# Reordering the products of a quantized gated feed-forward inside one large fused kernel

## The chip, the cores and the metric

The kernel runs on one core of a Trainium2 chip. The metric is the device time of one execution in microseconds. A core has five engines that run side by side, each through its own instructions in a fixed order: TensorE (PE in the profile) multiplies matrices into PSUM banks, VectorE (DVE), ScalarE (ACT) and GpSimd (POOL) work on elements, and SyncE (SP) issues transfers. An instruction that waits for another engine, or for a transfer, holds up everything that is queued behind it on its own engine.

## The reference

Two layers, each of a sequence mixer `s` and a feed-forward with `g = silu(ffn)`, joined as `x + s * g`, on x of 2 x 512 x 512 in float32. The change lies in the feed-forward of the second layer, and beside it lie small preparations for the second mixer (a state space model with 128 heads).

```python
Wg, Wu, Wd = dequant(gate_q, gate_s), dequant(up_q, up_s), dequant(down_q, down_s)
gate_score = silu(einsum('bsh,ih->bsi', x, Wg))          # h 512, i 1792
return einsum('bsi,hi->bsh', gate_score * einsum('bsh,ih->bsi', x, Wu), Wd)
...
xn = _layernorm(x)
s = _L1_attn_ref(xn, ...)       # its dt: softplus of a projection; cumulative sums over 128 steps
g = silu(_L1_ffn_ref(xn, ...))
x = x + s * g
```

`dequant` multiplies integers by a scale per group of 128 inputs. The mixer's last product takes `out_proj_w` with its rows scaled by `gnorm_w`.

## The kernel before, in words

The kernel runs layer 0, then the feed-forward of layer 1, then the mixer of layer 1. Layer 0 is put in order by a scheduler; from the line `ordered.enter_context(tc.manual_schedule())` on, each engine executes its instructions in the order in which the program writes them. At the seam the scheduler may place instructions of layer 0 between the first ones of the feed-forward: so it is with `second_input` for the second sequence (normalisation at L196, transposes `xn1t` at L133, copies at L134), which the second sequence's tiles need.

*The feed-forward.* The 1792 inner features are cut into four blocks of 512, 512, 512 and 256. A block has tiles of 128 features for each of the two sequences (b), and two tiles make a pair (q). `load_block` loads integers and scales of gate (g), up (u) and down (d) weights on SP's queue into a ring of six buffers, and its `finish` dequantises them on DVE (L549). The loops run (q, b) = (0,0), (0,1), (1,0), (1,1) in each block; in block 0 the pairs with q = 0 are computed by `single_tiles`, all others by `pair_of_tiles`. When the pairs of a block are done, eight `pf` tiles (L893, four 128-row tiles of each sequence) multiply by the down weights and are added up in `gl` (tiles `g`, L901 and L903).

*Plain tiles.* `single_tiles` (L816) makes four groups of 128x512 results (two tiles, g and u), each of four matmuls, then ACT takes silu (L823) and DVE the product (L824). The trace counts each float32 matmul twice.

*Pairs of tiles.* `pair_of_tiles` computes a pair for gate and for up with seven half-size products in place of eight (Winograd's form of Strassen's method). `seven` names them 1 to 7: factors are quarters of weights and activations and sums of them (`sg`, `su` by `weight_sums` and `th` by `column_sums`, all on POOL, L483 and L472). A product is two matmuls of 128x256 (L509, `product`). Of each kind one PSUM bank `ps` (names pg, pu) holds two sums: 1, 6, 7 and 4 are accumulated in the left half and 5 and 3 in the right; product 2 goes to a bank `py` shared by g and u. Quarters of the result are numbered c = 0 to 3 (tile c // 2, half of the columns c % 2). They are taken from the running sum: c = 0 is product 1 plus 2, c = 1 the sum after 6 plus the right half with 3, c = 3 the sum after 7 plus the right half, c = 2 the sum after 4. ACT copies the left half after 1, 6 and 7 (L777, L789); DVE adds (L782, L791, L797). Then ACT takes silu of gate (L801 to L803) and DVE multiplies by up (L806). The order on PE is 1 5 (g), 1 5 (u), 2 (g), add, 2 (u), add, 6 6, 7 7, then 4 3 (g), 4 3 (u).

*Work beside it.* `side` is called twice in a pair, at its two yields, and after every second `pf` tile. One call takes the next piece of `prepare` (for the mixer: `hn` and transposes `ht` with their copies to hT, the projection `pdt`, softplus by a polynomial on DVE L655 to L667, cumulative sums by matmul `cs`, `cj` and `ct`, exponentials on ACT) and the next two pieces of `scale_out`: SP loads 128 rows of `out_wT` into `wop` (L730), DVE scales (L735), POOL's queue writes to `wo_d` (L736). The three buffers of `wop` let a piece be scaled two pieces after its load.

*Behind it.* `load_bc(0)` loads the weights `wbc` of the mixer's first projection (`pjbc`, L1011) at the end of block 0, into a room of one buffer. After the last block SP loads `wh`, `wg` and `wo`, and `head` starts the mixer with `pjbc` and then `pjh`.

Of the kernel before, what the change touches and what calls it, by code (L numbers as in the profile page):

```python
# [15 lines left out]
P = 128  # L16
D = 512
# [31 lines left out]
def fused_kernel(  # L49
# [488 lines left out]
    with ExitStack() as l1:  # L538
# [33 lines left out]
        def prepare():  # L572
# [27 lines left out]
            for b in range(B):  # L600
# [55 lines left out]
                nc.vector.reciprocal(v, v)  # L656
                nc.vector.tensor_tensor(u, u, v, ALU.mult)
                nc.vector.tensor_tensor(q2, u, u, ALU.mult)
                nc.vector.tensor_scalar(v, q2, 1.0 / 17, None, ALU.mult)
                yield  # L660
                for n in range(15, 1, -2):
                    nc.vector.scalar_tensor_tensor(v, v, 1.0 / n, q2, ALU.add, ALU.mult)
# [4 lines left out]
                nc.vector.tensor_copy(part(0), grouped(z))  # L667
                Af = row("q2", "Af")
# [52 lines left out]
        def scale_out():  # L721

            pieces = [divmod(i, GT) for i in range(NG * GT)]
            ts = {}
            for i in range(len(pieces) + 2):
                if i < len(pieces):
                    g, k = pieces[i]
                    ts[i] = tmp.tile([P, D], F32, tag="wop", name=f"wop{i}", bufs=3)
                    o0 = g * GW + k * P
                    nc.sync.dma_start(ts[i], out_wT[o0 : o0 + P, :])  # L730
                if i > 1:
                    g, k = pieces[i - 2]
                    t = ts.pop(i - 2)
                    ct = g * GT + k
                    nc.vector.tensor_scalar(t, t, gn[:, ct : ct + 1], None, ALU.mult)  # L735
                    nc.gpsimd.dma_start(wo_d[g][:, k, :], t)  # L736
                yield
# [17 lines left out]

        def pair_of_tiles(its, sums, b, name):

            f = {kind: seven(*sums[kind], xn1T[b], b) for kind in "gu"}
            ps = {kind: bank(f"p{kind}{name}", (P, 2, HD)) for kind in "gu"}
            py = None  # L760
# [7 lines left out]
            def multiply(kind, i):  # L768
                if i == 2:
                    product(py["gu".index(kind)], f[kind][i], kind == "g")  # L770
                else:
                    product(ps[kind][:, int(i in (3, 5))], f[kind][i], i == 1)

            for kind in "gu":
                multiply(kind, 1)
                multiply(kind, 5)
                nc.scalar.copy(quarter(kind, 0), ps[kind][:, 0])  # L777
            two = bank(f"py{name}", (P, 2, HD))
            py = [two[:, 0], two[:, 1]]
            for kind in "gu":  # L780
                multiply(kind, 2)
                nc.vector.tensor_tensor(  # L782
                    quarter(kind, 0), quarter(kind, 0), py["gu".index(kind)], ALU.add
                )
            yield
            for i, c in ((6, 1), (7, 3)):
                for kind in "gu":
                    multiply(kind, i)
                    nc.scalar.copy(quarter(kind, c), ps[kind][:, 0])  # L789
                    if i == 7:  # L790
                        nc.vector.tensor_tensor(  # L791
                            quarter(kind, 3), quarter(kind, 3), ps[kind][:, 1], ALU.add
                        )
            for kind in "gu":
                multiply(kind, 4)
                multiply(kind, 3)
                nc.vector.tensor_tensor(  # L797
                    quarter(kind, 1), quarter(kind, 1), ps[kind][:, 1], ALU.add
                )

            nc.scalar.activation(its[1][:, 0:HD], ps["g"][:, 0], AF.Silu)  # L801
            nc.scalar.activation(its[1][:, HD:], its[1][:, HD:], AF.Silu)
            nc.scalar.activation(its[0], its[0], AF.Silu)  # L803
            for c in (2, 3, 0, 1):
                x = ps["u"][:, 0] if c == 2 else us[c]
                nc.vector.tensor_tensor(quarter("g", c), quarter("g", c), x, ALU.mult)  # L806
# [24 lines left out]
        def side():  # L831

            next(pieces, None)
            for _ in range(2):
                next(scaled, None)

        sums = {}
        for n, (i0, iw) in enumerate(blocks):
# [10 lines left out]
            for q in range(ni // 2):  # L849
                for b in range(B):  # L850
                    two, name = its[b][2 * q : 2 * q + 2], f"{i0}{q}{b}"
                    if n == 0 and q == 0:
                        run = single_tiles(two, q, b, name)
                    else:
                        run = pair_of_tiles(two, sums, b, name)
                    for half in range(2):
                        next(run)
                        if n > 0 or q > 0:
                            side()
                    for _ in run:  # L860
                        pass
                    if n == 0 and q == 0 and b == 0:
                        for s in range(B):
                            column_sums(s, xn1T[s])
                    if q == 0 and b == (1 if n == 0 else 0):
                        w["d"] = fin["d"]()
                        if more:
                            nxt["g"] = load_block("g", n + 1)
                    if q == 0 and b == 0 and ni > 2:
                        ahead = {kind: weight_sums(kind, 1, f"{i0}_1") for kind in "gu"}  # L870
# [909 lines left out]
```

## Time and profile before

| | us |
| --- | --- |
| median of 3 runs | 2334.16 (2332.72 to 2335.03) |
| the profiled execution | 2329.24 |
| its span, first to last instruction | 2327.5 |
| PE, DVE, ACT, POOL busy in it | 2255.4, 1433.8, 1247.8, 1134.7 |
| first matmul of the feed-forward (L816) | 243.14 |
| first plain tiles of the second sequence | 269.49 |
| first `pf` of blocks 0, 1, 2, 3 | 316.65, 415.73, 511.76, 565.75 |
| first `pjbc` | 580.42 |

Times in the trace count from the start of the span. A timeline line has start, length, engine, source line, operation, output <- input, shape, count, and in brackets how long the engine had been idle and what released it. The length of a matmul is modelled, and matmuls overlap: their pace is read from one start to the next. A line of the waits has the waiting operation, what it waited for, the total, how often, and the longest. The granted clock is TensorE's, 1.00 at full speed; over the whole span it was 0.993.

### The profile page before, as it was taken

Reading aid. Unit: us, or ns where it says so; the run is one execution under the profiler, and the core shown is the slowest. Engines: PE = TensorE matmul, PEld = TensorE weight load, DVE = VectorE, ACT = ScalarE, POOL = GpSimd, SP = SyncE. Lnnn points to the kernel's source line nnn. Section 1 sums busy time; section 2 is a strip of 40 time slices with the busy share of each in tenths; the row PEclk is TensorE's granted clock in tenths of the full one; section 3 lists DMA queues with packets and bytes.
Section 4 is the critical chain, followed back from the end, with each engine's and each line's share of the span. In section 5 each row is a group of like instructions: output and inputs, shape, how many; then the busy total and the mean of one; then the engine's idle time right before and its main releaser. Section 6 shows DMA issues by size and latency. Waiting matters only on the chain.

```text
span 2327.5 us, 33414 instructions
## 1 busy us (share of the span) xinstructions
PE 2255.4 (97%) x11804; PEld 1598.1 (69%) x11804; DVE 1433.8 (62%) x2766; ACT 1247.8 (54%) x2688; POOL 1134.7 (49%) x995
## 2 busy tenths in 40 slices
PE   7989898999999999999999999999999999999998
PEld 4545457665557777777777777777777777777776
DVE  5263456643676666666667666666666676757663
ACT  3141224222676666666666575656666665666660
POOL 4151522233164554745654474547465554655475
PEclk9999999999999999999999999999999999999999
DMA  4021255564454444444544354544445454444452
GB/s 165 0 73 54 80 172 187 206 232 170 144 180 139 143 135 154 123 127 137 185 130 129 118 160 136 152 155 136 118 127 174 133 152 123 159 118 135 147 158 91
DMA packets 195510, 323.38 MB, mean 139 GB/s; under 512 B 17680, under 2 KB 129168, under 8 KB 192912
## 3 DMA queue, kind: packets, MB, share of 16 engines
q1 hardware_dynamic: 188944, 300.28, 42.3%
q0 software_dynamic: 6400, 20.98, 2.4%
q8 instruction: 94, 1.54, 0.3%
q14 instruction: 72, 0.59, 0.1%
HBM read 294.45 MB, written 26.74 MB: 138 GB/s over the span
## 4 chain that ended last, share of the span: by engine, by line
PE 87%; DVE 6%; ACT 4%; DMA 1%; issue 1%; POOL 1%; SPq 0%; DVEq 0%; ACTq 0%
PE pjh L1011 18%; PE of L1334 14%; PE gt L509 12%; PE py L1041 5%; PE pjbc L1011 5%; PE pn L1139 4%; PE pf L893 3%; PE py L1050 3%; PE sh L415 2%; PE pg L509 2%; PE ofy L1334 2%; PE gty L509 2%; PE px L1093 2%; PE gt L1011 2%; PE hu L304 2%; PE pu L509 2%
## 5 line engine op out<-in xcount | busy, mean ns | idle before, releaser
L1011 PE MATMUL pjh<-hT,wh 128*128 128x512 f32 x1024 | 467.5, 599 | 0.5
L1157 POOL TENSOR_TENSOR eb<-CT,eb 128x768 f32<-128x768 f32 x128 | 230.2, 1818 | 443.4 <-DMA eb<-ea_d 416.1
L1022 DVE SCALAR_TENSOR_TENSOR hid<-pjh,cw,hid 128x511 f32<-128x511 f32 (+2 forms) x384 | 286.9, 747 | 83.2 <-ACT hid L1017 74.1
L1011 PEld LDWEIGHTS pjh<-hT,wh 128*128 128x128 f32 x1024 | 187.8, 190 | 202.5 <-issue 200.3
L1117 ACT ACTIVATE cs<-cs,sl 128x128 f32<-128x128 f32 x1024 | 323.6, 388 | 1.0 <-DMA cs<-cs_d 1.0
L483 POOL TENSOR_TENSOR sw<-wg 128x256 f32<-128x256 f32 x114 | 84.1, 738 | 287.7 <-PE gt L509 287.6
L1132 DVE TENSOR_TENSOR cs<-de,CB 128x512 f32<-128x512 f32 x256 | 175.4, 685 | 77.2 <-ACT de L1131 77.2
L1017 ACT ACTIVATE hid<-pjh,cb,cw 128x512 f32<-128x512 f32 x128 | 99.2, 775 | 166.3 <-PE pjh L1011 166.3
L1131 ACT ACTIVATE de<-cs 128x512 f32<-128x512 f32 x256 | 154.0, 602 | 49.3 <-DVE cs L1132 43.2
L1041 PE MATMUL py<-cs,hc 128*64 128x128 f32 x2048 | 180.3, 276 | 0.0
L1348 DVE SCALAR_TENSOR_TENSOR acc<-of,rg,acc 128x256 f32<-128x256 f32 x192 | 92.1, 481 | 137.8 <-PE of L1334 137.1
L509 PE MATMUL gt<-th,sw 128*128 128x256 f32 x684 | 175.6, 379 | 0.0
L1461 POOL TENSOR_TENSOR y<-y,sgt 128x512 f32<-128x512 f32 x124 | 161.9, 1327 | 12.1 <-ACT sgt L1217 9.9
L1086 POOL TENSOR_TENSOR sums<-sums,sq 128x512 f32<-128x512 f32 x110 | 140.1, 1274 | 19.4 <-ACT sq L1082 15.7
L1050 PE MATMUL py<-eb,st 128*64 128x128 f32 x1536 | 149.1, 273 | 0.0
L1145 DVE SCALAR_TENSOR_TENSOR st<-st,sl,pn 128x64 f32<-128x64 f32 x512 | 103.8, 275 | 62.5 <-ACT st L1141 62.4
L509 PEld LDWEIGHTS gt<-th,sw 128*128 128x128 f32 x684 | 126.7, 190 | 21.4 <-issue 6.5
L1041 PEld LDWEIGHTS py<-cs,hc 128*64 128x64 f32 x2048 | 121.5, 137 | 15.4 <-issue 13.4
L736 POOL DMA_DIRECT2D wo_d<-wop x64 | 34.7, 546 | 196.1 <-DVE wop L735 195.7
L1070 DVE SCALAR_TENSOR_TENSOR y<-hid,Dcol,y 128x512 f32<-128x512 f32 x128 | 125.7, 982 | 4.5
L1334 PE MATMUL of<-wt,y 128*128 128x256 f32 x512 | 120.6, 379 | 0.0
L1206 ACT COPY sgt<-gt 128x256 f32<-128x256 f32 x171 | 63.4, 371 | 104.6 <-PE gt L509 104.6
(330 smaller groups left out, 4586.2 us busy)
## 6 DMA issues: line engine op xcount, KB each, us to landing
cs<-cs_d SPq DMA_DIRECT2D x128, 512.0 KB, 4.2
eb<-ea_d SPq DMA_DIRECT2D x256, 192.0 KB, 6.1
wh<-in_in_wT SPq DMA_DIRECT2D x64, 512.0 KB, 9.1
wg<-in_in_wT SPq DMA_DIRECT2D x64, 512.0 KB, 7.5
el<-ea_d SPq DMA_DIRECT2D x256, 128.0 KB, 7.5
wop<-in_out_wT SPq DMA_DIRECT2D x64, 256.0 KB, 2.8
wo_d<-wop POOLq DMA_DIRECT2D x64, 256.0 KB, 2.6
wo<-wo_d SPq DMA_DIRECT2D x16, 1024.0 KB, 8.7
```

Source lines behind the costliest of these rows:

```text
L509: nc.tensor.matmul(ps, x[:, k, :], y[:, k, :], start=(first and k == 0), stop=(k == 1), skip_group_check=True,)
L1011: nc.tensor.matmul(ps, w_of(k), hT[:, k, bass.ts(b, S)], start=(k == 0), stop=(k == KD - 1))
L1022: nc.vector.scalar_tensor_tensor(dst[:, j:], ps[:, : S - j], cw[:, ct, KCONV - 1 - j : KCONV - j], dst[:, j:], ALU.mult, ALU.add,)
L1041: nc.tensor.matmul(py[bass.ts(hh, HP), bass.ts(c, P)], hc[:, c, bass.ts(hh, HP)], M[:, hh, bass.ts(c, P)], start=True, stop=(c == 0),)
L1050: nc.tensor.matmul(py[bass.ts(hh, HP), bass.ts(c, P)], st[:, c - 1, bass.ts(hh, HP)], cte[:, hh, bass.ts(c - 1, P)], start=False, stop=True,)
L1086: nc.gpsimd.tensor_tensor(sums[u], sums[u], q, ALU.add)
L1117: nc.scalar.activation(m[:, bass.ts(c, P)], m[:, bass.ts(c, P)], AF.Relu, bias=sls[g][:, 3, b * NCH + c, h0 + hh : h0 + hh + 1], scale=-1.0,)
L1131: nc.scalar.activation(pe, m, AF.Exp, scale=-1.0)
L1132: nc.vector.tensor_tensor(m, pe, CBs[s // GT].rearrange("p c i -> p (c i)"), ALU.mult)
L1157: nc.gpsimd.tensor_tensor(eb_t[s], CTs[s // GT][:, P:].unsqueeze(1).to_broadcast([P, 2, S - P]), eb_t[s], ALU.mult,)
L1334: nc.tensor.matmul(ps, x[:, k, :], y[:, k, :], start=(first and k == 0), stop=(k == 3), skip_group_check=True,)
L1461: nc.gpsimd.tensor_tensor(y_of(s), y_of(s), sgs.pop(s), ALU.mult)
```

## The change

Products: 2 (g) and 2 (u) now follow each other, and 6 follows, before the adds that take `py`. Product 3 of a pair, with its add and the silu and multiply of quarter 1, moves into the next pair: its g part behind that pair's product 6, its u part behind its product 7. After a block's last pair both stand behind the first `pf` tile. Silu is taken quarter by quarter.

Order: block 0 runs (0,0), (1,0), (0,1), (1,1), with (1,0) computed by `single_tiles` too. The dequantisations of block 0's down weights and of block 1's gate weights now both stand behind (0,1).

Beside it: a pair has four yields, `side` is called at each and after every `pf` tile, and takes one piece of `scale_out` instead of two. `prepare` yields at more places. `scale_out` has five buffers, of which two lie in the room of `wbc`, and scales a piece four calls after its load. `load_bc(0)` moves to the end of the last block. Block 0's `column_sums` and `weight_sums` follow (1,0).

```diff
-                yield
                 for n in range(15, 1, -2):
+                    if n % 4 == 3:
+                        yield
                     nc.vector.scalar_tensor_tensor(v, v, 1.0 / n, q2, ALU.add, ALU.mult)
...
+            room = tmp.tile([P, 3, D], F32, tag="wop", name="wop")
+            more = wa.tile([P, KD, 2, NST], F32, tag="wbc", name="wop_more", bufs=1)
+            more = more.rearrange("p k j o -> p (k j o)").rearrange("p (i d) -> p i d", i=2)
+            slots = [room[:, i] for i in range(3)] + [more[:, i] for i in range(2)]
+            behind = len(slots) - 1
+            for i in range(NG * GT + behind):
+                if i < NG * GT:
+                    o0 = i * P
+                    nc.sync.dma_start(slots[i % len(slots)], out_wT[o0 : o0 + P, :])
+                if i >= behind:
+                    ct = i - behind
+                    t = slots[ct % len(slots)]
                     nc.vector.tensor_scalar(t, t, gn[:, ct : ct + 1], None, ALU.mult)
+                    g, k = divmod(ct, GT)
                     nc.gpsimd.dma_start(wo_d[g][:, k, :], t)
                 yield
...
+            def gated(c, dst=None):
+                q = quarter("g", c)
+                nc.scalar.activation(q, ps["g"][:, 0] if c == 2 else q, AF.Silu)
+                nc.vector.tensor_tensor(q, q, ps["u"][:, 0] if c == 2 else us[c], ALU.mult)
             for kind in "gu":
                 multiply(kind, 1)
                 multiply(kind, 5)
+                copy(kind, 0)
+            yield
             two = bank(f"py{name}", (P, 2, HD))
             for kind in "gu":
-                multiply(kind, 2)
-                nc.vector.tensor_tensor(
-                    quarter(kind, 0), quarter(kind, 0), py["gu".index(kind)], ALU.add
-                )
+                multiply(kind, 2, two[:, "gu".index(kind)])
+            for kind in "gu":
+                multiply(kind, 6)
+                copy(kind, 1)
+            for kind in "gu":
+                add(kind, 0, two[:, "gu".index(kind)])
+            gated(0)
+            if late:
+                late[0]()
             yield
+            for kind in "gu":
+                multiply(kind, 7)
+                copy(kind, 3)
+            if late:
+                late[1]()
+            late.clear()
+            for kind in "gu":
+                add(kind, 3)
+            yield
             for kind in "gu":
                 multiply(kind, 4)
+            gated(2)
+            gated(3)
+            def last(kind):
+                multiply(kind, 3)
+                add(kind, 1)
+                if kind == "u":
+                    gated(1)
+            late.extend([lambda: last("g"), lambda: last("u")])
             yield
...
+            order = [(q, b) for q in range(ni // 2) for b in range(B)]
             if n == 0:
+                order = [(0, 0), (1, 0), (0, 1), (1, 1)]
+            for q, b in order:
+                two, name = its[b][2 * q : 2 * q + 2], f"{i0}{q}{b}"
+                if n == 0 and (q, b) != (1, 1):
+                    run = single_tiles(two, q, b, name)
+                else:
+                    run = pair_of_tiles(two, sums, b, name)
+                for _ in run:
+                    if n > 0 or b > 0:
+                        side()
...
             if more:
                 ahead = sums = {kind: weight_sums(kind, 0, f"{i0}_2") for kind in "gu"}
             else:
+                wbc = {0: load_bc(0)}
                 wh = {q: load_hid(q) for q in range(2)}
...
-                    if r % 2 == 1:
-                        side()
+                    if b == 0 and r == 0:
+                        for f in late:
+                            f()
+                        late.clear()
+                    side()
```

## The prediction, on record before the result was known

> **What bounds the kernel now.** I read the page first (which engine is full, and which chain ends last), then the stage that the change touches, then what TensorE (PE) waits for there, then the two engines side by side around one such wait.
>
> The page's busy table and its chain that ended last:
>
> ```profile
> PE 2255.4 (97%) x11804; PEld 1598.1 (69%) x11804; DVE 1433.8 (62%) x2766; ACT 1247.8 (54%) x2688; POOL 1134.7 (49%) x995
> ...
> PE 87%; DVE 6%; ACT 4%; DMA 1%; issue 1%; POOL 1%; SPq 0%; DVEq 0%; ACTq 0%
> ```
>
> PE is the bound; DVE and ACT are on the chain only where PE stood waiting for them. The change touches only the quantized ffn, 243.14 us (first L816 matmul) to 579.64 us (end of the last L893). Busy time by stage of that stretch:
>
> ```profile
> 243.20:265.10 21.90, 13.85 (x34) 5.87 (x32) 19.92 (x31) 6.58 (x10) 14.72 (x12) 0.93 0.35 117
> ...
> 283.40:316.00 32.60, 27.08 (x116) 22.23 (x114) 14.14 (x30) 13.49 (x31) 2.17 (x4) 0.95 0.34 112
> 316.00:348.60 32.60, 32.60 (x113) 17.25 (x112) 21.14 (x32) 2.54 (x3) 10.14 (x14) 1.00 0.59 195
> 348.60:446.80 98.20, 90.58 (x386) 65.74 (x385) 64.00 (x118) 29.25 (x61) 26.93 (x40) 0.98 0.57 201
> 446.80:539.20 92.40, 84.94 (x337) 60.56 (x336) 44.69 (x90) 20.52 (x46) 26.98 (x42) 0.98 0.63 213
> ```
>
> Columns: stretch, its length, then busy us of PE, PE's weight loads, DVE, ACT, POOL, then granted clock and DMA. PE is short of its stretch, DVE is at two thirds. The ends of matmuls are modelled, so the loss is larger than these gaps. At its undisturbed pace a product of 128x256 takes a slot of 0.864 us (539.23 to 540.09 below), so a pair of 14 takes 12.10; a plain tile-kind 3.43; the eight `pf` tiles 27.47 (13.74 in the last block); hT transposes 3.46 in all, pdt 7.1, cs, cj and ct 10.7, xn1t 1.9. Before: 8 x 3.43 + 12 x 12.10 + 96.2 + 3.5 + 7.1 + 10.7 + 1.9 = 292.1 of 336.5 us. **44.4 us are excess**, and only that can be won. What PE waited for there:
>
> ```profile
> PE py L509 <- DVE it L782: 17.3, 12, 4.8
> PE xn1t L133 <- DVE acc L196: 8.1, 1, 8.1
> PE pg L509 <- DVE it L791: 3.7, 2, 2.7
> ```
>
> Twelve waits at `py` (one a pair), one for the second sequence's normalisation. An undisturbed pair, then a disturbed one, on PE:
>
> ```profile
> 539.23 1.03 PE L509 MATMUL pg<-xn1T,w_g 128*128 128x256 f32 x4
> 540.09 1.03 PE L509 MATMUL pg<-th,sg 128*128 128x256 f32 x4
> ...
> 542.68 1.03 PE L509 MATMUL py<-xn1T,w_g 128*128 128x256 f32 x4
> 544.29 1.13 PE L509 MATMUL py<-xn1T,w_u 128*128 128x256 f32 x4 [0.58 <-DVE it L782]
> ```
> ```profile
> 489.50 1.03 PE L509 MATMUL pu<-th,w_u 128*128 128x256 f32 x4
> 493.26 1.20 PE L509 MATMUL pg<-th,w_g 128*128 128x256 f32 x4 [2.74 <-DVE it L791]
> 494.26 1.91 PE L509 MATMUL pg<-xn1T,sg 128*128 128x256 f32 x4
> 495.96 1.84 PE L509 MATMUL pu<-th,w_u 128*128 128x256 f32 x4
> ```
>
> Even undisturbed, a pair takes 13.26 us (539.23 to 552.49), 1.16 over 12.10: 0.75 before the second `py` product and the rest at products 7 and 4. In the disturbed one the add that PE needs was queued on DVE behind two scalings that waited for their DMA:
>
> ```profile
> 487.18 0.42 DVE L782 TENSOR_TENSOR uq<-uq,py 128x256 f32<-128x256 f32 x1 [1.29 <-PE py L509]
> 491.34 0.49 DVE L735 TENSOR_SCALAR wop<-wop,gn 128x512 f32<-128x512 f32 x1 [3.74 <-DMA wop<-in_out_wT]
> 492.30 0.58 DVE L735 TENSOR_SCALAR wop<-wop,gn 128x512 f32<-128x512 f32 x1 [0.48 <-DMA wop<-in_out_wT]
> 492.81 0.40 DVE L791 TENSOR_TENSOR it<-it,pg 128x256 f32<-128x256 f32 x1
> ```
>
> So DVE's order, not its load, is the loss.
>
> **The change, part by part.**
>
> *First block.* (1,0) is computed plainly ahead of the second sequence: 13.73 us for a pair of 13.26. The instruction order of the changed kernel shows that only three of its sixteen matmul groups (3 x 0.86 = 2.6 us) come ahead of the xn1t transposes; PE arrives there at 256.87 + 2.6 = 259.4 and `acc` is unchanged at 265.1. The wait falls from 8.05 to 5.6 only, the 0.67 us wait for xn1T goes. Three groups of tiles end at 293.35 instead of 296.59: **-3.2**.
>
> *Pair order.* In the new pair both product-2 matmuls stand before the adds, so the 0.75 at `py` goes. Product 3 of the previous pair is put after 6 (g) and after 7 (u). That widens 6 to 7 and 7 to 4 by a slot. But DVE executes in order, and between 7 and 4 stand: add(u,1) of the previous pair (waits for 3u), its multiply, and only then add(g,3), for which 4g waits as it did before (L791 above). From the end of 3u's slot: DVE starts 0.20 later (399.66 to 399.86), add 0.46 to a dependent multiply (342.51 to 342.97, same length), 0.34 to an independent add (464.24 to 464.58), add 0.42, back to PE 0.05, restart 0.10: **about 1.5 us before 4g in every pair with a predecessor**, against 1.16 before. There are seven such pairs (three each in blocks 1 and 2, one in block 3); the first pair of a block pays 0.2, and its own product 3 goes into `pf`, where POOL's and SP's queues don't matter to it. I found no row of before with this order, so bounds: 0 if DVE takes add(g,3) unhindered, 3.7 if a scaling in the pieces ahead of it waits for DMA as at 491.34. I take 1.5, the sum of nearest rows.
>
> *Preparation in finer pieces, one scaling a call.* Pieces now come four times a pair and once a `pf` tile, before add(0), before add(u,1), before multiply(2) and at the end. What lies before add(0) has some 4.4 us of cover (product 2's adds aren't needed until copy 3, five slots on). What lies before add(u,1) has 2.2 us (end of 3g to end of 3u); beyond that it is PE's. Followed by hand with the rows of before (512-wide: tensor_tensor 0.69, scalar_tensor_tensor 0.72 each, reciprocal 3.35, scaling 0.44, dequantisation 2.28, hn 0.44, hT 0.64; ACT copy 0.37, four squares 2.45, table load 1.28):
> - block 0, last pair: sqrt of the first preparation, two dequantisations (4.56) and hn ahead of the first hT transpose: excess 2.0. All of v's chain falls under `pf`, with reciprocal and polynomial between `g` copies; six banks cover it. Before 296.59 to 348.57 = 52.0; now 12.1 + 1.7 + 3.6 + 27.5 + 2.0 = 46.8. **-5.2**.
> - block 1: pair (0,0) with cs, cj, ct: 0.3. (0,1): ACT has squares and two table loads ahead of copy(g,0), and hn behind the dequantisation: 3.3. (1,0): u, q2, v and a scaling, 2.3 us, in the narrow place: 3.0. (1,1): 1.5. The 3.0 gap also cools PE (below): 1.7. Sum 9.8 in place of 11.7: **-2.0**, unrounded. The second sequence's cs, cj, ct (5.35) move from block 2 into this `pf`; that is taken out of both sides.
> - block 2: 0.2 + 3 x 1.5 = 4.7 in place of 11.2 (2.80 and 2.74 waits, 1.7 cold): **-6.5**.
> - block 3: 1.7 for 2.5: **-0.8**.
>
> *Five buffers.* Load to scaling is now four calls instead of two half as dense ones. A slot's cycle is POOL issue 0.54, write 2.6, load 2.8, about 6 us, against four calls of about 3 us: the DMA wait on DVE should go (counted in block 2). Price: the weights `wbc` of the next stage share the room, so their two loads (8.6 us) move on SP's queue from block 0 to the end, behind the last scaling's write (call 68 of 78). That is at about 12 us into the last pair; they land some 7 us ahead of their first use (the `pf` of 13.7 plus product 3 follow). Behind them on SP wait `wh`, `wg` and `wo`; `wh0` is used 7 us after `wbc`, `wh1` waits for product 3 anyway, 19 us ahead of use. So nothing, and one us for each us if those 7 are used up. POOL's issues are as many as before.
>
> Sum -3.2 - 5.2 - 2.0 - 6.5 - 0.8 = **-17.7**: of the profiled execution's 2329.24 (span 2327.5) 2311.5 remain. The median of the runs is 4.9 above that execution, so **2316.5**.
>
> [...] After the 2.74 us gap, two products took 1.91 and 1.84 for 1.03: with the third 1.7 us lost, as after gaps of 4.83 and 3.30; after one of 2.80 nothing. [...] I take the rows. [...]
>
> **Rivals.**
> - *No gap before 4g* (DVE gets through add(g,3) in time): seven times 1.5 less, 2306.0. For it: DVE is at two thirds. Against it: its order in the built program.
> - *ACT and DVE hold each other*: silu(0), which waits for DVE's adds, now stands on ACT before copy(g,3); formerly all silus came last. One us more in each of eleven pairs: 2327.5. For it: block 1's DVE 64 of 98 us, in lumps. Against: five slots of slack.
> - *Slower*: the scaling before add(u,1) waits for its DMA in every late pair. At 2.5 us a time (17.7 / 7) the gain is gone, past 3.2 it is a loss; with 491.34's 3.74 each, 26.2 more: 2342.7. Against it: the 6 us cycle above in four calls.
> - *No change*: gaps merely move, 2334; only with both of the middle ones.
>
> **How the numbers follow.** Forecast 0.58, no gap 0.13, hold each other 0.18, slower 0.06, no change 0.05. The forecast's own range is 2310 to 2322 (0.9 us a late pair either way, the cold array, the wait for acc). Leaving out the far ends of the other cases gives 2305 to 2327. A measurement of this kernel tells about 0.2% (4.7 us) from no change: faster 0.88, same 0.06, slower 0.06.
>
> **What would show it.** Right: a wait of 5 to 6 us before xn1t; none for `py`; about 1.3 us shown before 4g (the `pg` product from `th`, after product 3u) released by DVE's add; wop scalings without DMA waits; the last `pf` ending 17 to 18 us earlier, `pjbc` following it within 1 us. Wrong: `pjbc` waiting for `wbc`, ACT copies releasing products 6 or 4, or 4g's waits well over 1.5 in block 2.

## The result, and the profile after

| | before | after |
| --- | --- | --- |
| median of 4 runs each, side by side (us) | 2333.44 (2331.70 to 2335.03) | 2318.32 (2316.73 to 2320.97) |
| ratio, with its 95% interval | 1 | 0.9936 (0.9919 to 0.9954) |
| profiled execution, span | 2329.24, 2327.5 | 2317.27, 2315.5 |
| the stage: first plain matmul to first `pjbc` | 337.28 | 324.36 |

The changed kernel is faster, by 15.1 us in the medians. In the profiled executions 12.0 us are gained: 12.9 in the stage, less 1.0 outside it.

Busy engines, and the head of the chain that ended last, on the page of the changed kernel:

```profile
PE 2249.6 (97%) x11780; PEld 1591.5 (69%) x11780; DVE 1434.6 (62%) x2758; ACT 1248.2 (54%) x2693; POOL 1135.3 (49%) x995
...
PE 89%; DVE 5%; ACT 4%; POOL 1%; issue 1%; DMA 0%; SPq 0%; DVEq 0%; ACTq 0%; POOLq 0%
```

DVE's and DMA's parts of the chain shrank by a point each, and nothing new entered it. The four blocks of the changed kernel follow (stretch, length, busy us of PE, weight loads, DVE, ACT and POOL, clock, DMA), and below them the list of what PE waited for:

```profile
243.65:341.27 97.62, 90.53 (x281) 49.20 (x280) 60.42 (x96) 26.67 (x46) 41.65 (x44) 0.97 0.42 139
341.27:444.10 102.83, 93.74 (x433) 70.33 (x432) 65.43 (x118) 35.22 (x74) 28.43 (x41) 1.00 0.65 221
444.10:526.95 82.85, 76.80 (x290) 54.38 (x288) 35.80 (x75) 15.49 (x41) 26.15 (x40) 1.00 0.58 192
526.95:568.01 41.06, 38.57 (x146) 27.00 (x144) 19.27 (x37) 11.62 (x28) 18.00 (x22) 1.00 0.53 183
```
```profile
PE pg L509 <- DVE it L785: 13.4, 10, 3.0
PE xn1t L133 <- DVE acc L196: 5.5, 1, 5.5
PE ht L626 <- DVE hn L619: 3.9, 5, 1.5
PE pg L509 <- ACT it L781: 1.2, 1, 1.2
```

The same cut of the kernel before has blocks of 105.43, 98.21, 92.45 and 41.19 us. The second sequence's `cs`, `cj` and `ct` (5.35 us of matmuls) lay in block 2 and now lie in block 1, so like for like the gains are 7.8, 0.7, 4.3 and 0.1 us. The wait for `py`, 17.3 us before, is gone. In its place ten waits stand ahead of product 4 (L785 is `add`), and these had been two. The end of a pair in block 2, on PE and then on DVE:

```profile
491.73 1.03 PE L509 MATMUL pg<-th,w_g 128*128 128x256 f32 x4
492.60 1.03 PE L509 MATMUL pu<-th,w_u 128*128 128x256 f32 x4
493.46 1.03 PE L509 MATMUL pu<-xn1T,su 128*128 128x256 f32 x4
495.95 1.10 PE L509 MATMUL pg<-th,w_g 128*128 128x256 f32 x4 [1.47 <-DVE it L785]
```
```profile
494.52 0.42 DVE L785 TENSOR_TENSOR uq<-uq,pu 128x256 f32<-128x256 f32 x1 [1.58 <-PE pu L509]
495.05 0.42 DVE L791 TENSOR_TENSOR it<-it,uq 128x256 f32<-128x256 f32 x1
495.39 0.42 DVE L785 TENSOR_TENSOR it<-it,pg 128x256 f32<-128x256 f32 x1
```

The third DVE line is add(g,3), which product 4 needs. Its own inputs were ready after product 7 of the gate; in front of it stand the previous pair's add(u,1), which waits for the moved product 3 (493.46), and that pair's multiply. This is the order that the prediction read off the program. Between the first matmuls of two such pairs lie 13.79 us.

### The profile page after: what moved, and what is told of

It is laid out like the page before. It is cut to its first block, busy times and chain, and to the rows that moved or that the text cites. A ratio compares the mean times of both kernels' runs of the same rounds, so it can differ in the third digit from the quotient of the medians.

```text
span 2315.5 us, 33350 instructions
## 1 busy us (share of the span) xinstructions
PE 2249.6 (97%) x11780; PEld 1591.5 (69%) x11780; DVE 1434.6 (62%) x2758; ACT 1248.2 (54%) x2693; POOL 1135.3 (49%) x995
## 4 chain that ended last, share of the span: by engine, by line
PE 89%; DVE 5%; ACT 4%; POOL 1%; issue 1%; DMA 0%; SPq 0%; DVEq 0%; ACTq 0%; POOLq 0%
PE pjh L1037 18%; PE of L1360 14%; PE gt L509 12%; PE py L1067 5%; PE pjbc L1037 5%; PE pf L916 4%; PE pn L1165 4%; PE py L1076 3%; PE sh L415 2%; PE ofy L1360 2%; PE gty L509 2%; PE px L1119 2%; PE pg L509 2%; PE pu L509 2%; PE gt L1037 2%; PE hu L304 2%
## 5 line engine op out<-in xcount | busy, mean ns | idle before, releaser
L1487 POOL TENSOR_TENSOR y<-y,sgt 128x512 f32<-128x512 f32 x124 | 161.9, 1327 | 12.4 <-ACT sgt L1243 10.5
L1095 DVE TENSOR_TENSOR y<-py,el 128x512 f32<-128x512 f32 x128 | 87.7, 685 | 51.7 <-PE py L1076 51.7
```

The lines of the kernel that those rows point to most:

```text
L1487: nc.gpsimd.tensor_tensor(y_of(s), y_of(s), sgs.pop(s), ALU.mult)
```

## Experiments

Whole times of different kernels differ by up to 8 us outside the stage, where their work is the same: span less stage is 1990.2 us before, 1991.1 after, 1997.9 in the first experiment. Of the 7.7 us between the kernel before and the first experiment 3.1 lie ahead of the stage (its first matmul at 246.19 for 243.14) and 4.7 behind it, where over the last 146 us of the span TensorE's granted clock is 0.98 in the one and 0.94 in the other. So each mechanism is judged on the length of the stage in the trace, with the whole time beside it. A stage length is one execution's, and matmuls at about half pace behind a wait (called cold below, the others warm) move it by 1.6 to 4.7 us from kernel to kernel. (In the kernel before, behind the wait of 4.83 us, two products started 1.71 us apart for 0.86, and the granted clock from 307 to 309 us was 0.50. In the experiments cold is said of the products' lengths and starts.) A difference of that size is told by the waits and not by the length alone. Each timed kernel ran beside the kernel before on its own chip; the ratio is to that. The changed kernel's ratio has the interval 0.9919 to 0.9954; those of experiments 1, 3, 4, 8 and 9 overlap it, so that their whole times alone don't part them from it.

**1. Adds of product 7 ahead of the late ones.** In the changed kernel only the order on DVE:

```diff
             for kind in "gu":
                 add(kind, 3)
+            if late:
+                late[2]()
+            late.clear()
...
-                add(kind, 1)
-                if kind == "u":
-                    gated(1)
+                if kind == "g":
+                    add(kind, 1)
+            def rest():
+                add("u", 1)
+                gated(1)
```

> Changed kernel, but on DVE the two adds of quarter 3 stand before the previous pair's add and multiply of quarter 1 (PE's order is untouched). Theory (the 1.47 us before product 4 come from DVE's order): the wait goes in block 2's three late pairs and block 3's one (4 x 1.6 = 6.5 us) and shrinks by about 0.9 in each of block 1's three; 2309, and no wait of PE for add(g,3) over 0.5 us in block 2's late pairs. Rival (DVE is simply too loaded there): 2318, the same waits.

Measured: 2313.70 us, ratio 0.9913 (0.9898 to 0.9928). The stage is 315.76 us, 8.6 less than after, and the pairs of block 2 with a predecessor come 12.09 us apart instead of 13.79. The waits of PE in this kernel, the first line of which had 13.4 us:

```profile
PE xn1t L133 <- DVE acc L196: 5.5, 1, 5.5
PE pg L509 <- DVE it L785: 4.2, 4, 2.0
PE ht L626 <- DVE hn L619: 3.9, 5, 1.5
PE pg L509 <- ACT it L781: 1.2, 1, 1.2
```

So the gap of the late pairs is DVE's order and nothing else. Of the stage's gain 4.6 us reached the median, which lies between the two expectations. The stretches outside the stage took more time here, as said above.

**2. The old order of block 0**, with everything else of the change left in (block 1's gate weights are dequantised behind (1,0) again):

```diff
-                order = [(0, 0), (1, 0), (0, 1), (1, 1)]
+                order = [(0, 0), (0, 1), (1, 0), (1, 1)]
-                if n == 0 and (q, b) != (1, 1):
+                if n == 0 and q == 0:
```

> Changed kernel, but block 0 in the order of before, (0,0), (0,1), (1,0), (1,1), the last two as pairs; preparation starts with (1,0). Theory: the wait before the transposes is 8.0 instead of 5.5 and 0.7 for their copies returns (+3.2), (1,0) takes 12.5 instead of 13.7 (-1.2), (1,1) has a late product 3 before it (+1.6): 2322. Rival (the order is of no account): 2317 to 2319.

Measured: 2339.57 us, ratio 1.0023 (1.0011 to 1.0034), a miss: slower than before. The stage is 343.50 us, and 18.3 of the 19.1 us over the changed kernel are block 0 (115.89 us). PE and DVE of this run, at the first of four waits of 3.9 to 5.4 us, two in block 0 and two in block 1:

```profile
297.43 2.07 PE L509 MATMUL pg<-th,w_g 128*128 128x256 f32 x4 [5.35 <-DVE it L785]
```
```profile
295.17 0.17 DVE L106 TENSOR_SCALAR ssh<-ssh 128x4 f32<-128x4 f32 x1 [1.92 <-ACT jkh L613]
296.69 0.18 DVE L108 RECIPROCAL ssh<-ssh 128x4 f32<-128x4 f32 x1 [1.35 <-ACT ssh L107]
296.95 0.42 DVE L785 TENSOR_TENSOR it<-it,pg 128x256 f32<-128x256 f32 x1
```

The preparation's square root, a chain between ACT and DVE, is inside a pair and stands ahead of the add that product 4 waits for. In the changed kernel the same chain begins beside a plain group, whose results nobody waits for so soon. (2.6 us of the loss are the wait before `xn1t`, which is 8.0 us again.)

**3. Product 3 back in its own pair**, ahead of the pair's end, all else left in:

```diff
-            late.extend([lambda: last("g"), lambda: last("u")])
+            for kind in "gu":
+                last(kind)
```

> Changed kernel, but product 3 with its adds and silu stays at the end of its own pair; product 2, pieces, buffers and block 0 as changed. Theory: a late pair takes 12.1 + 0.45 instead of 13.79, seven times 1.25 less: 2309.5; moving product 3 costs what the rest of the change wins. Rival (the moved product is what covers the copies and adds): products 7 and 4 wait again and it is slower than the changed kernel, 2322 to 2328.

Measured: 2319.87 us, ratio 0.9943 (0.9928 to 0.9958); stage 325.71 us. Neither expectation held. Blocks 2 and 3 gained 2.9 and 1.2 us, in the direction of the first (the last two pairs of block 2 take 12.6 us, its first two 14.1 and 13.2), but block 1 lost 5.7 us. There PE waited 1.81 us for a silu on ACT ahead of product 3, and 3.44 us ahead of product 4, and cold products of up to 2.07 us followed. Starts that lie 1.28 to 1.87 us apart for 0.86 make 4.7 of the 5.7 us. So this run doesn't show what the moved product is worth in block 1: that it fills waits there is likely, but most of the loss lies in cold products.

**4. The second sequence's transposes behind its turn.** `xn1t` of that sequence is taken out of `second_input` at the end of layer 0 and put behind (1,0), where PE has plain tiles to do until the normalisation is ready:

```diff
+                    for r in range(NCH):
+                        rt = (B - 1) * NCH + r
+                        features(acc[rt], xn1T[B - 1][:, :, bass.ts(r, P)], f"xn1t{rt}")
                     for s in range(B):
                         column_sums(s, xn1T[s])
```

> Changed kernel, but the four transposes of the second sequence and their copies are issued after all of (1,0) instead of within it. Theory: the wait of 5.5 us and the 1.8 us of cold clock behind it go, 0.7 us for the copies returns: 2311.7. Rival (what follows then waits for the transposed activations and their sums on POOL): 2316 to 2319.

Measured: 2315.65 us, ratio 0.9924 (0.9909 to 0.9938); stage 321.31 us. Block 0 gained 6.35 us, as expected, but block 1 gave 3.3 back, and the whole time lies between the two expectations. PE's waits in block 1 are the same ones; what differs is the pace of the products behind them. Two of its products in block 1 of this kernel, then the second one in the changed kernel:

```profile
368.62 2.04 PE L510 MATMUL pg<-th,w_g 128*128 128x256 f32 x4 [0.95 <-DVE it L786]
...
389.18 2.04 PE L510 MATMUL pg<-th,w_g 128*128 128x256 f32 x4 [2.99 <-DVE it L786]
391.02 1.76 PE L510 MATMUL pu<-th,w_u 128*128 128x256 f32 x4
```
```profile
393.96 1.10 PE L509 MATMUL pg<-th,w_g 128*128 128x256 f32 x4 [2.99 <-DVE it L785]
394.90 1.03 PE L509 MATMUL pu<-th,w_u 128*128 128x256 f32 x4
```

**5. Both edits, 1 and 4.**

> The two edits that each gained alone, together: in every pair the adds of products 7 stand on VectorE ahead of the second add and the multiply of the pair before, and the transposes of the second sequence's input stand behind its plain tiles. If the two gains are of different places (waits of 1.1 us before product 4 in blocks 2 and 3 here, the 5.5 us wait of the transposes there) they add: the stage from the first plain tile to the last product of the ffn measured 324.4 us in the changed kernel, 315.8 and 321.3 with the one and the other edit, and the second's own gain in block 0 was 6.4 us, of which block 1 gave 3.3 back through colder products; together 309.4 us if block 1 gives nothing back and 312.7 us if it gives the same back. The whole time is then 2303 to 2311 us, the width being the last 146 us, which scattered by 4 us between kernels that are the same there. Rival: the waits are covers of each other, and the stage stays at 315 us or more.

Measured: 2303.24 us, ratio 0.9864 (0.9847 to 0.9880). The stage is 307.69 us, even below the 309.4 expected: the two gains are of different places, and block 1 gave nothing back. It is 1.6 us shorter than in experiment 1, where the same wait of 2.04 us was followed by cold products. Experiment 1, and then this one:

```profile
394.71 1.29 PE L509 MATMUL pg<-th,w_g 128*128 128x256 f32 x4 [2.04 <-DVE it L785]
395.79 1.91 PE L509 MATMUL pu<-th,w_u 128*128 128x256 f32 x4
```
```profile
385.40 1.13 PE L510 MATMUL pg<-th,w_g 128*128 128x256 f32 x4 [2.04 <-DVE it L786]
```

**6. The same, and silu and multiply of quarter 0 behind the adds of product 7.**

```diff
             for kind in "gu":
                 add(kind, 0, two[:, "gu".index(kind)])
-            gated(0)
...
             for kind in "gu":
                 add(kind, 3)
+            gated(0)
             if late:
                 late[2]()
```

> As the one with both edits, and the silu and the multiply of quarter 0 moved behind the adds of products 7. In the first pair of block 2 that multiply stood on VectorE ahead of the add that product 4 waits for, and waited itself for a silu behind a table load of 1.28 us (wait before product 4 there 1.65 us); if that is the cause, this wait goes, and the one of 2.0 us in block 1's third pair, where the silus of the pair stand in the same place, falls by 0 to 1.5 us: the stage is 1.6 to 3.2 us shorter than with both edits alone, about 307 us. Rival: the wait is of ScalarE's copies for product 7, and stays; the stage is the same within 0.5 us.

Measured: 2300.61 us, ratio 0.9855 (0.9840 to 0.9870), the fastest kernel of this study and well under the changed one, whose interval it doesn't touch. The stage is 305.47 us, 2.2 less. Block 2 gave 1.6 of it, where the first pair went from 12.28 us to 10.68. In block 1 the third pair's wait fell from 2.04 to 0.69 us, but in the second pair product 6 now waits 3.23 us for a copy of ACT instead of 1.16, with a product of 2.07 us behind it, and block 1 as a whole stayed the same, 99.5 us for 99.3. So in block 2 the multiply was the cause, and not ACT's copies as the rival had it; in block 1 a wait for ACT, with the cold products behind it, took back what had been gained.

**7. One line alone: both products 2 ahead of their adds**, in the kernel before:

```diff
             for kind in "gu":
                 multiply(kind, 2)
+            for kind in "gu":
                 nc.vector.tensor_tensor(
```

> The kernel before with one line of the change alone: both products 2 of a pair stand ahead of their two adds, so that the second product does not wait for the add of the first, which reads the other half of the same bank. The kernel before waits 17.3 us in all for py; by hand, what is not met again by the next wait is 4.0 us in block 0, 2.3 in block 1, 2.4 in block 2 and 1.5 in block 3, 10 us in all: 2323 to 2325 us. It would mean that the larger part of what the change gains comes from this order alone. Rival: the adds then end as late as they did, and the waits only move on to products 7 and 4: 2331 to 2334 us.

Measured: 2332.18 us, ratio 0.9982 (0.9971 to 0.9992); stage 334.74 us, 2.5 less than before. The rival is right: the wait moved on. PE's waits for `py` are gone and stand ahead of product 4 instead. The list of this run, and then DVE ahead of the longest one:

```profile
PE pg L509 <- DVE it L792: 20.0, 6, 7.0
PE xn1t L133 <- DVE acc L196: 8.1, 1, 8.1
```
```profile
491.06 0.49 DVE L735 TENSOR_SCALAR wop<-wop,gn 128x512 f32<-128x512 f32 x1 [6.70 <-DMA wop<-in_out_wT]
492.00 0.49 DVE L735 TENSOR_SCALAR wop<-wop,gn 128x512 f32<-128x512 f32 x1 [0.45 <-DMA wop<-in_out_wT]
492.40 0.42 DVE L792 TENSOR_TENSOR it<-it,pg 128x256 f32<-128x256 f32 x1
```

DVE stood 25.7 us in all for the transfers of pieces, against 9.2 before. Why is not shown; that the scalings are reached sooner when PE is through products 2 sooner is the author's guess.

**8. The changed kernel with three buffers** for the pieces:

```diff
-            slots = [room[:, i] for i in range(3)] + [more[:, i] for i in range(2)]
+            slots = [room[:, i] for i in range(3)]
```

> The changed kernel with three buffers for the pieces of the output weights where it has five, each scaled two calls after its load. From load to scaling there are then about 10 us in the pairs' pace, against a transfer of 6 us or so in the trace; VectorE waits for a piece where a pair's calls come closer, and the adds behind it come late by as much: 2319 to 2323 us, if the five buffers do anything. Rival: with one piece a call the transfers are landed anyway, and the time is that of the changed kernel, 2318 us (within 1.5).

Measured: 2324.87 us, ratio 0.9953 (0.9939 to 0.9968); stage 328.51 us, 4.2 more. The median is above what either view expected, but its ratio's interval overlaps the changed kernel's. DVE waits 8.2 us for pieces, in five places, yet PE's waits are those of the changed kernel within 0.4 us (13.5, 5.5, 4.3 and 1.2 us). Of the 4.2 us 3.4 are in block 1, and they follow the same waits of 0.95 and 3.00 us, with products of 1.94 and 2.04 us behind them where the changed kernel has 1.10. So beside pieces that come one a call, five buffers took nothing off PE's waits. Most of the difference in the stage is one of that pace; whether the buffers have a part in how it fell was not tested. (A piece lands 2.8 us after its issue in the kernel before, in the median, and 2.8 or 2.9 in the changed one, where the expectation has 6.)

**9. Both products 2 ahead, and five buffers**, in the kernel before: experiment 7 with `scale_out` of the change, two pieces still scaled in a call, and `load_bc(0)` at the end.

```diff
+            slots = [room[:, i] for i in range(3)] + [more[:, i] for i in range(2)]
+            behind = len(slots) - 1
...
             for kind in "gu":
                 multiply(kind, 2)
+            for kind in "gu":
                 nc.vector.tensor_tensor(
```

> The kernel before with both products 2 ahead of their adds, and with five buffers for the output weights' pieces, two pieces still scaled in one call. With the order of products 2 alone the wait only moved: PE waited 20.0 us before product 4, and ahead of three of those six waits VectorE stood for a transfer of a piece (2.30, 3.89 and 6.70 us). If those transfers are what the gain was lost to, the five buffers give them two calls more to land, these three waits (4.19, 2.84 and 7.01 us) fall by 9 to 13 us with the colder products behind them, the stage goes from 334.7 to 322 to 326 us, and the time to 2320 to 2324 us. Rival: the two scalings and the multiplies ahead of the add of product 7 fill VectorE anyhow; the waits fall by less than 5 us, and the time is 2328 us or more.

Measured: 2314.94 us, ratio 0.9905 (0.9889 to 0.9922); stage 319.05 us. The buffers gained 15.7 us on top of the 2.5 of the product's order, more than the 9 to 13 us expected. The two together are already at least as good as the whole change (0.9905 against 0.9936). The buffers without the product's order were not run, and `load_bc(0)` moved with them, so how the 18.2 us are shared is not shown. No wait of DVE for a piece is left. PE's list has two waits of 5.8 us for DVE ahead of product 4 in place of six of 20.0:

```profile
PE xn1t L133 <- DVE acc L196: 8.0, 1, 8.0
PE pg L509 <- DVE it L793: 5.8, 2, 4.8
```

**10. The order of block 0 alone**, in the kernel before: (1,0) as plain tiles ahead of the second sequence, with the pairs, pieces and buffers as they were. As in the change, block 1's gate weights are loaded behind (0,1) and dequantised there at once, where the kernel before had a pair in between.

```diff
-            for q in range(ni // 2):
-                for b in range(B):
+            order = [(q, b) for q in range(ni // 2) for b in range(B)]
             if n == 0:
+                order = [(0, 0), (1, 0), (0, 1), (1, 1)]
```

> The kernel before with one part of the change alone: the first sequence's tiles of block 0 ahead, three plain groups, and one pair in that block; pairs, pieces and buffers as before. The changed kernel without this part was 21 us slower than with it, where the prediction gave the part 3.2 us and the shorter wait of the transposes. If the part is worth that much by itself, because preparation then begins beside plain tiles, which wait for nobody on VectorE: 2313 to 2318 us. If it is worth that only together with the finer pieces (which run into the pairs without it): 2328 to 2331 us, as the prediction's sum had it, 2331 minus up to 2.5 us for the transposes. Block 0's length in the trace tells: 105.4 us before, 97.6 us in the changed kernel, 115.9 us in the changed kernel without the part.

Measured: 2343.16 us, ratio 1.0033 (1.0024 to 1.0043): a miss of both, slower by 8 us. Stage 347.40 us, block 0 111.55. SP's queue (start, length until the last of the group was issued), DVE and PE of this run show how:

```profile
271.81 28.70 SPq L730 DMA_DIRECT2D wop<-in_out_wT  x4
300.61 0.38 SPq L545 DMA_DIRECT2D q_g<-in_gate_qT  x1
301.08 0.46 SPq L546 DMA_DIRECT2D w_g<-in_gate_sT  x1
```
```profile
309.18 2.29 DVE L549 TENSOR_TENSOR w_g<-q_g,w_g 128x2048 f32<-128x2048 int32 x1 [9.10 <-DMA w_g<-in_gate_sT]
311.39 0.41 DVE L782 TENSOR_TENSOR it<-it,py 128x256 f32<-128x256 f32 x1
```
```profile
311.86 2.08 PE L509 MATMUL py<-xn1T,w_u 128*128 128x256 f32 x4 [13.60 <-DVE it L782]
```

Four loads of pieces are issued beside (0,1), for three buffers. The fourth waits for the first to be scaled and written, and block 1's gate weights, which are behind it on SP, are asked for at 300.61 instead of 272.94 as in the changed kernel. DVE waits for their scales, and PE for DVE.

**11. Parts 7, 9 and 10 together:** products 2, five buffers and the order of block 0, with neither product 3 moved, nor pieces finer, nor silu in quarters.

```diff
+            order = [(q, b) for q in range(ni // 2) for b in range(B)]
             if n == 0:
+                order = [(0, 0), (1, 0), (0, 1), (1, 1)]
...
+            slots = [room[:, i] for i in range(3)] + [more[:, i] for i in range(2)]
...
+            for kind in "gu":
                 nc.vector.tensor_tensor(
```

> The kernel before with three parts of the change: products 2 ahead of their adds, five buffers, and the first sequence's tiles of block 0 ahead. With three buffers that last part cost 10 us, and the trace of that run shows where: on the DMA queue of SP the fourth load of a piece stood 28.7 us for a free buffer, and the load of block 1's gate weights behind it, so that VectorE stood 9.1 us for the weights' scales and TensorE 13.6 us for VectorE. With five buffers the four loads of that stretch find room. If that was all, block 0, 101.4 us with the two other parts, gains 2.6 us at the transposes (wait of 8.0 us to 5.5) and up to 1.7 us at the last pair's waits, and pays 1.6 us for a plain group where a pair was: 97.5 to 99.5 us, and the time is 2311 to 2313 us. Rival: the part costs by itself (preparation begins later and runs into block 1's pairs): block 0 at 101 us or more or block 1 longer by over 3 us, the time 2315 us or more.

Measured: 2311.58 us, ratio 0.9900 (0.9883 to 0.9916); stage 314.72 us, block 0 97.03. As expected (block 0 came out 0.5 us under its range): with room for the pieces, the order that cost 10.1 us of stage alone gains 4.3.

**12. The same, with the transposes of experiment 4.**

> The kernel before with the same three parts, and the transposes of the second sequence's input behind its plain tiles: the best that was found without moving product 3 and without finer pieces, to set against the best with them (2300.6 us, stage 305.5 us, which has the adds of products 7 ahead and the multiply later besides). The transposes gained 6.4 us in block 0 in the changed kernel; here the same: stage 308.4 us, 2302 to 2306 us. If it comes to that, moving product 3 and the finer pieces are worth no more than 3 us even where they are mended. Rival: what the transposes gain is given back in block 1 through colder products, as it was in the changed kernel (3.3 us): stage about 311.5 us, 2305 to 2310 us.

Measured: 2304.91 us, ratio 0.9878 (0.9861 to 0.9896); stage 308.65 us, as expected, with block 0 5.9 us shorter and nothing given back.

The stage lengths in one table, each from one profiled execution:

| kernel | block 0 | 1 | 2 | 3 | stage |
| --- | --- | --- | --- | --- | --- |
| before | 105.43 | 98.21 | 92.45 | 41.19 | 337.28 |
| products 2 (7) | 104.33 | 96.40 | 94.51 | 39.50 | 334.74 |
| and five buffers (9) | 101.36 | 95.73 | 82.46 | 39.50 | 319.05 |
| and block 0's order (11) | 97.03 | 95.73 | 82.47 | 39.49 | 314.72 |
| and the rest: the change | 97.62 | 102.83 | 82.85 | 41.06 | 324.36 |
| and adds first (1) | 97.72 | 100.96 | 77.73 | 39.35 | 315.76 |
| and late transposes (5) | 91.28 | 99.32 | 77.73 | 39.36 | 307.69 |
| and the multiply later (6) | 90.70 | 99.46 | 76.14 | 39.17 | 305.47 |

(In the rows from the change on, 5.35 us of `cs`, `cj` and `ct` lie in block 1 instead of block 2.)

Three of the change's parts make 22.6 us of gain, and the rest takes 9.6 back, of which the order on DVE that experiment 1 mends is 8.6. Where product 3 stays at home, pairs take 12.41 us in experiments 9 and 11, so the gap that it was moved to cover is 0.3 us once DVE is free; moved, they take 13.79. (Cold products have a part in these sums: behind the wait of 4.81 us in block 1, experiments 9 and 11 have them, the first of 2.01 and 1.95 us, while the changed kernel has none in block 1.) Mended, with the adds first, the rest comes to about nothing (315.76 against 314.72; with late transposes 307.69 against 308.65).

## Why the prediction was right, and where it was not

The forecast was 2316.5 us and the median is 2318.3, for the predicted reason, but the agreement is a little luckier than the working. The prediction took 17.7 us off the stage and 4.9 us from the profiled execution to the median. The stage gave 12.9, the rest of the program cost 1.0, and the median lay 1.1 above its profiled execution. Errors of 4.8 and 1.0 us one way and 3.9 the other leave 1.9.

*Pair order.* Right in kind and size: no wait for `py`, and a gap before product 4 of the gate (4g) in all seven late pairs. It measured 1.69 us a pair in block 2 (13.79 less 12.10) where the prediction took 1.5 (the rows that it lists add up to 1.57). Experiment 1 shows the cause, DVE's queue: with the adds ahead, those pairs take 12.09 us. The rival without a gap put 10.5 us on it; with that one order changed the stage came 8.6 us shorter and the median to 2313.7.

*The first pair of a block.* Mis-sized: 0.2 us was predicted and block 2's first pair lost 1.9 (12 products of 0.864 are 10.37, the pair took 12.28). With 0.19 more in each of the three late pairs this is all that is missing in block 2: 4.3 us gained, 6.5 predicted. Block 3 has the same two terms, at 0.1 us gained for 0.8: its first pair lost 0.5 us, its late pair 1.7, and its pairs before had lost 2.3 us where 2.5 were counted. In block 2, ACT of the changed kernel, then DVE, then PE:

```profile
451.60 1.28 ACT L790 ACT_TABLE_LOAD   x1
```
```profile
453.34 0.43 DVE L791 TENSOR_TENSOR it<-it,uq 128x256 f32<-128x256 f32 x1 [3.04 <-ACT it L790]
453.69 0.48 DVE L738 TENSOR_SCALAR wop<-wop,gn 128x512 f32<-128x512 f32 x1
454.08 0.41 DVE L785 TENSOR_TENSOR it<-it,pg 128x256 f32<-128x256 f32 x1
```
```profile
454.55 1.13 PE L509 MATMUL pg<-th,w_g 128*128 128x256 f32 x4 [1.65 <-DVE it L785]
```

The multiply of quarter 0 waits for a silu, whose table ACT has just had to load, and add(g,3) is queued behind it. The stage has 18 table loads, each of 1.28 us, where the kernel before has 17. The prediction named ACT's order as a rival, one us in each of eleven pairs; it did not follow the multiply into DVE's queue, ahead of the add. Experiment 6 moved it, and that pair came to 10.68 us.

*Block 0.* 7.8 us for the 8.4 of two steps. The sum was right, but what it gives for one part holds only beside the others. The loop order, costed at 3.2 us, is worth 4.3 of stage on top of experiment 9, minus 10.1 alone, and 19.1 inside the finished change. The prediction looked at PE's side of that step. The 10.1 us lost come from SP's queue, which had no free buffer (experiment 10), and the 19.1 from preparation that stands inside pairs on DVE (experiment 2), so the step can't be costed without the buffers and without where preparation starts. The wait before `xn1t` was right, 5.5 us for 5.6; experiment 4 shows that the whole of it was to be had.

*Block 1.* 0.7 us gained for 2.0. Pair by pair over its undisturbed length: (0,0) 0.5 for 0.3, (0,1) 5.6 for 3.3, (1,0) 3.2 for 3.0, (1,1) 1.7 for 1.5, and the 1.7 us of a cold array did not come. So (0,1) was 2.3 us short. While POOL makes the sums of the next weights, DVE's work there took longer than the rows that the step was costed with. In the changed kernel, DVE and POOL:

```profile
364.20 2.29 DVE L549 TENSOR_TENSOR w_d<-q_d,w_d 128x2048 f32<-128x2048 int32 x1
366.40 1.83 DVE L619 TENSOR_SCALAR hn<-acc,ssh 128x512 f32<-128x512 f32 x2
368.16 0.94 DVE L738 TENSOR_SCALAR wop_more<-wop_more,gn 128x512 f32<-128x512 f32 x1
```
```profile
365.14 1.95 POOL L483 TENSOR_TENSOR sg<-w_g 128x256 f32<-128x256 f32 x1
367.16 0.78 POOL L483 TENSOR_TENSOR sg<-sg,w_g 128x256 f32<-128x256 f32 x1
```

Two `hn` took 1.83 us for 0.88 and a scaling 0.94 for 0.48; with a multiply (0.75 for 0.42) and the next two `hn` (1.23 for 0.88), that is 2.1 us more of DVE. The size fits what is missing. How much of it reached PE was not tested, and so the cause of this term stays argued.

*The buffers.* "Nothing, and the DMA wait counted in block 2" was right for the change: no scaling waits for its transfer any more, `wbc` was issued at 549.5 and `pjbc` does not wait for it. But the step gave the buffers no weight of their own. In the kernel before, the product order is worth 2.5 us without them and the two are worth 18.2 together; in the changed kernel, where pieces come one a call, PE's waits are the same with three buffers (experiment 8).

*Cold products and tables.* The prediction charged 1.7 us for block 1's gap of 3.0 us. In the changed kernel nothing came of it: the two products behind 2.99 us took 1.10 and 1.03 us, at a granted clock of 1.00. In two others (experiments 4 and 8) the charge fits: gaps of 2.99 and 3.00 us were followed by products of 2.04 us, then 1.76 or 1.82, and gaps of 0.95 us by products of 2.04 and 1.94, where the changed kernel has 1.10. A gap of 2.04 us was followed by cold products in experiment 1 (1.29, then 1.91 us) and by a warm one in experiment 5 (1.13). So the length of one gap did not decide it here; what did is not shown. For ACT's tables the prediction's 1.28 us held: in the changed kernel the load at 362.20 took 1.28 us and the next function began at 363.50.

*The rivals.* In the late pairs of blocks 2 and 3, DVE does wait for ACT's silu, but early enough: what PE waits for there is the moved product 3. One such wait, which is over before that product ends:

```profile
491.79 0.43 DVE L791 TENSOR_TENSOR it<-it,uq 128x256 f32<-128x256 f32 x1 [1.62 <-ACT it L790]
```

In two places, where ACT has a table to load, such waits reach PE: before product 6 in block 1 (1.2 us) and before product 4 in block 2's first pair (1.65 us). A transfer that DVE waits for in every late pair did not come.

## What to carry to other kernels

A wait that is taken from the busiest engine can move on to the next thing that its supplier has queued: before an edit is costed, write down what stands between the supplier's last input and the result that is waited for, in the supplier's own order, its waits for third engines included. Put the operations that the busy engine needs first, and those of the previous tile, multiplies and weight pieces behind them; that was worth 8.6 us of stage here. And test parts in combination: the order of block 0 alone cost 10 us and gained 4 or 19 beside others. Alone, it made a DMA queue stand 28.7 us for a free buffer, with every load behind it held; in the finished change it kept preparation out of the pairs, where DVE's adds are waited for.

## What the runs showed of the hardware

Identical stalls had different ends. The same wait of 2.99 or 3.00 us before the same product left TensorE warm in one kernel (1.10 and 1.03 us, at a granted clock of 1.00) and cold in two (2.04, then 1.76 or 1.82). In experiment 4 the cold products behind such a gap and one of 0.95 us come to 3.3 us of stage, more than many an edit here, so a gain of that size, read from whole times or from one stage length, may come from cold products alone.

In the changed kernel's stage, VectorE's scaling of a 128x512 tile took 0.94 to 0.96 us in four places where GpSimd was adding weights, 0.62 in a fifth, and 0.39 to 0.48 everywhere else. GpSimd's first addition took 1.94 to 1.95 us in the four series that began while VectorE was dequantising a 128x2048 tile, and 0.73 in the first series, where VectorE stood idle. VectorE's adds that read PSUM took 0.41 to 0.42 beside these additions as elsewhere. What the cause is was not tested.
